# Filter spectra in DRAM: eight frequencies stored inside each lag, one 8 KB piece per Toeplitz row

## The chip, the cores and the metric

The kernel runs on one core of one Trainium2 chip. The metric is device time in microseconds of the whole launch; the median of three runs of the kernel before is 2986.34 us. TensorE is called PE below, VectorE DVE, ScalarE ACT, GpSimd POOL and SyncE SP. DMAs are issued from the queues of SP, POOL and ACT, and sixteen DMA engines move the bytes.

## The reference

Two layers act on `x` of shape (2, 128, 64, 64), that is two samples of 4096 tokens with 128 channels.

- Layer 0: group norm, a 1x1 projection to q, k and v with 2-D rotary positions, attention with four heads over 4096 tokens, an output projection and a residual.
- Layer 1, first half: `t = t + softmax(n n^T) n` with `n = layernorm(t)`.
- Layer 1, second half, where the change lies: a spectral filter. Cut to its core:

```python
Vf = rfft(phi, n=8192, axis=0)                      # 16 filters over 4096 lags
U_plus  = irfft(Vf * rfft(u))[:4096]                # causal convolution, per filter and channel
U_minus = irfft(Vf * rfft(u * sign))[:4096] * sign
out = einsum('btkd,k,kde->bte', U_plus,  s, Mpp) + einsum('btkd,k,kde->bte', U_minus, s, Mpm)
out = out + sum_i  shift(u, i) @ M_u[i]             # three taps
t = t + out                                         # of the branch that the softmax picks
```

## The kernel before, in words

Layer 0 and the attention of layer 1 run first, up to about 1740 us. In the attention of sample 0 (`attend(0, ...)`, 1030 to 1390 us), small pieces of other work are stepped beside the score loop by a chain of generators: statistics, then `filters`, then `matrices`, then `normalise` of sample 1. Beside the attention of sample 1 runs `feed` of sample 0.

`filters16` computes the spectra. For each parity `s` of the lags it transforms the filters to 128 frequencies with two matmuls, and DVE fills a tile `tb` of 128 frequencies by 2 (high and low half-precision part `h`) by 2 (row kind `i`) by 992 values: 31 lags of 32 values each. The tile is stored to the DRAM tensor `tables16` by one DMA on SP (L893), with the frequency outermost. `tb` uses a buffer tag "raw" that has one buffer, so the second parity's `tb` can be written only when the first one's store has read it; the raw matrices `mu_raw` and every second `raw` tile of `matrices` come next in that same buffer.

The filter stage takes the rest of the run. It works on 64 steps: 2 samples, 2 output parities `ro`, 8 chunks `ch` of 16 frequencies, 2 lag parities `s`. A step has two halves of `NS` = 8 frequencies. For each half, `chunk16` loads a table tile `tt` and a token tile `ut`, both of 128 partitions. Their partitions are filled in eight groups of 16 (four `q`, two `ci`): eight DMAs of 128 KB on SP for `tt` (L1311) and eight of 32 KB on POOL for `ut` (L1319). A table DMA builds the Toeplitz structure by itself: partition number p of the group reads 16 lags beginning at lag p, so neighbouring partitions read almost the same bytes, and one partition gets eight pieces (one for each frequency) of 1 KB.

`convolve16` multiplies: 16 matmuls per step of 128 x 128 by 128 x 512, the weights from `ut` and the moving operand `tt[:, at, :]` (L1372). ACT makes a half-precision copy of each result (L1379) and DVE the remainder (L1380). `mix16` (L1388) multiplies these with the mixing matrices, 48 matmuls per step, and is stepped one step behind. Matmuls of this stage stay in the order written (`ordered`). Table tiles exist twice (even steps `tables_a`, odd steps `tables_b`), token tiles twice per half. So the loads of step n wait until the matmuls of step n-2 have read the tile.

SP takes its DMAs strictly in order. In the first 16 steps `feed` of sample 1 shares its queue (stores `rows<-uh` at L1168 and L1169, which wait for ACT and DVE, and `base<-oc` at L1150), and in the later steps `back` (loads `had<-base` at L1484, which wait for the DVE additions at L1502). The framework also gives SP's DMAs eight semaphores in rotation: a DMA waits for the one issued eight before it to land, so at most eight of SP's are under way. POOL has eight of its own.

Apart from what is pinned, the framework orders each engine's instructions at build time by a plan with its own durations; a changed DMA can so move instructions elsewhere.

Of the kernel before, what the change touches and what calls it, by code (L numbers as in the profile page):

```python
# [13 lines left out]
F16 = mybir.dt.float16  # L14
# [8 lines left out]
P = 128  # L23
# [11 lines left out]
NK = 16  # L35
# [3 lines left out]
BP = NI // 2  # L39
NF = P  # L40
NW = NF // 4
NDI = 2 * BP - 1
TROW = NDI * NK
DROWS = 2 * BP + 1
WC = 4
NCH = NW // WC

# [25 lines left out]
def conv_attn_hybrid(ctx: ExitStack, tc: tile.TileContext, io):  # L75
    nc = tc.nc

    const = ctx.enter_context(tc.tile_pool(name="const", bufs=1))
    dram = ctx.enter_context(tc.tile_pool(name="dram", bufs=1, space=bass.MemoryType.DRAM))
# [27 lines left out]
    def pool(stack, name, bufs=1, **kw):  # L107
        return stack.enter_context(tc.tile_pool(name=name, bufs=bufs, reuse_waits="tile", **kw))
# [593 lines left out]

    tables = dram.tile([NF, 2, 2, 2 * TROW], F32, name="tables")
    rows = [dram.tile([2, DROWS, NF, C], F32, name=f"rows{b}") for b in range(B)]
    tables16 = dram.tile([NF, 2, 2, 2, 2 * TROW], F16, name="tables16")
    rows16 = [dram.tile([2, DROWS, 2, NF, C], F16, name=f"rows16_{b}") for b in range(B)]

    base = [dram.tile([C, NI, P], F32, name=f"base{b}") for b in range(B)]
# [42 lines left out]
    def network(layer0, in_halves):  # L751
        with ExitStack() as st:
            layers(st, layer0, in_halves)

    def layers(st, layer0, in_halves):
# [4 lines left out]
        px = pool(st, "px", side="right")  # L760
# [86 lines left out]
        def filters(p, fw):  # L847
            phi = p.tile([P, 2, TROW], F32, tag="phi", name="phi")
            nc.sync.dma_start(phi, io["phi"])
            yield  # L850
            if in_halves:
                yield from filters16(p, fw, phi)
                return
            for s in range(2):
                tb = p.tile([P, 2, 2 * TROW], F32, tag="raw", name=f"tb{s}")
                tbr = tb.rearrange("w i (o c k) -> w i c o k", c=2, k=NK)
                for c in range(2):
                    ph = bank(f"ph{s}_{c}")[:, :TROW]
                    nc.tensor.matmul(ph, fw[:, c, :], phi[:, s, :], start=True, stop=True)
                    ph = ph.rearrange("w (o k) -> w o k", k=NK)  # L860
                    nc.vector.tensor_copy(tbr[:, 0, c], ph)
                    if c == 0:
                        nc.vector.tensor_copy(tbr[:, 1, 1], ph)
                    else:
                        nc.vector.tensor_scalar(tbr[:, 1, 0], ph, -1.0, None, ALU.mult)
                    yield
                nc.sync.dma_start(tables[:, s], tb)

        def filters16(p, fw, phi):

            most = p.tile([P, 4, NK], F32, name="phi_most")
            for s in range(2):
                tb = p.tile([P, 2, 2, 2 * TROW], F16, tag="raw", name=f"tb{s}")
                tbr = tb.rearrange("w h i (o c k) -> w h i c o k", c=2, k=NK)
                for c in range(2):
                    ph = bank(f"ph{s}_{c}")[:, :TROW]
                    nc.tensor.matmul(ph, fw[:, c, :], phi[:, s, :], start=True, stop=True)
                    nc.vector.tensor_reduce(
                        most[:, 2 * s + c, :], ph.rearrange("w (o k) -> w k o", k=NK), AX.X, ALU.max,
                        apply_absolute_value=True,  # L880
                    )
                    ph = ph.rearrange("w (o k) -> w o k", k=NK)
                    nc.vector.tensor_scalar(tbr[:, 0, 0, c], ph, T_SCALE, None, ALU.mult)
                    nc.vector.scalar_tensor_tensor(
                        tbr[:, 1, 0, c], ph, T_SCALE, tbr[:, 0, 0, c], ALU.mult, ALU.subtract
                    )
                    for h in range(2):
                        if c == 0:
                            nc.vector.tensor_copy(tbr[:, h, 1, 1], tbr[:, h, 0, 0])
                        else:  # L890
                            nc.vector.tensor_scalar(tbr[:, h, 1, 0], tbr[:, h, 0, 1], -1.0, None, ALU.mult)
                    yield
                nc.sync.dma_start(tables16[:, s], tb)  # L893
            each = p.tile([P, NK], F32, name="phi_each")
            nc.vector.tensor_reduce(each, most.rearrange("p n k -> p k n"), AX.X, ALU.max)
            yield
            pt = bank("phi_most")
            nc.tensor.transpose(pt[:NK, :P], each, ident)
            col = p.tile([NK, 1], F32, name="phi_col")
            nc.vector.reduce_max(col, pt[:NK, :P], axis=AX.X)  # L900
            yield
            pt = bank("phi_row")
            nc.tensor.matmul(pt[0:1, :NK], col, ident[:NK, :NK], start=True, stop=True)
            ends = p.tile([1, 2], F32, name="phi_ends")
            nc.vector.tensor_reduce(ends[:, 0:1], pt[0:1, :NK], AX.X, ALU.max)
            nc.vector.tensor_reduce(ends[:, 1:2], pt[0:1, :NK], AX.X, ALU.min)
            nc.vector.tensor_scalar(ranges[:, 3:4], ends[:, 0:1], 1.0 / T_MOST, None, ALU.mult)
            nc.vector.tensor_scalar(ranges[:, 4:5], ends[:, 1:2], -1.0, 1.0 + T_LEAST, ALU.mult, ALU.add)
            yield
# [366 lines left out]
        late_pool = pool(right1, "late", 2, side="right")  # L1276

        if in_halves:
            pair = px.tile([P, 2, NF // NCH // 2, 2 * BP * NK], F16, tag="a", name="tables_a")
            tables_in = [  # L1280
                [pair[:, 0], pair[:, 1]],
                [px.tile([P, NF // NCH // 2, 2 * BP * NK], F16, tag=f"b{n}", name=f"tables_b{n}") for n in range(2)],
            ]
        else:
            tables_in = [
                px.tile([P, 2, WC // 2, 2 * BP * NK], F32, tag=f"b{n}", name=f"tables_in{n}") for n in range(2)
            ]

        def ordered(instruction):
            return tc.keep_in_program_order(instruction)  # L1290
# [4 lines left out]
        STREAM = {(0, 0): 0, (0, 1): 2, (1, 0): 1, (1, 1): 0}  # L1295
        FIRST = (0, BP + 1, BP)

        NS = NF // NCH // 2

        def chunk16(n, b, ro, ch, s):  # L1300

            row = FIRST[STREAM[ro, s]]
            halves = []
            for half in range(2):
                w0 = 2 * NS * ch + NS * half
                tt = tables_in[n % 2][half]
                ut = pf.tile([P, NS, C], F16, tag=f"tokens{half}", name=f"tokens{half}_{n}", bufs=2)
                for q in range(4):
                    for ci in range(2):
                        part = slice(32 * q + BP * ci, 32 * q + BP * ci + BP)  # L1310
                        nc.sync.dma_start(  # L1311
                            tt[part, :, :],
                            bass.AP(
                                tensor=tables16.tensor,
                                offset=tables16.offset + (((w0 * 2 + s) * 2 + q % 2) * 2 + ci) * 2 * TROW,
                                ap=[[2 * NK, BP], [16 * TROW, NS], [1, 2 * BP * NK]],
                            ),
                        )
                        nc.gpsimd.dma_start(  # L1319
                            ut[part, :, :], rows16[b][ci, row : row + BP, q // 2, w0 : w0 + NS, :]  # L1320
                        )
                halves.append((tt, ut))
            return halves
# [39 lines left out]
        def convolve16(u, halves, xh, xl):  # L1363

            for w in range(WC):
                tt, ut = halves[w // 2]
                pus = []
                for g2 in range(2):
                    pu = pc.tile([P, 2, 512], F32, tag="cv", name=f"cv{u}_{w}_{g2}", bufs=3)
                    for h in range(2):  # L1370
                        at = 4 * (w % 2) + 2 * g2 + h
                        ordered(nc.tensor.matmul(pu[:, h, :], ut[:, at, :], tt[:, at, :], start=True, stop=True))  # L1372
                    pus.append(pu)
                yield
                for g2, pu in enumerate(pus):
                    at = 128 * w + 64 * g2
                    pur = pu.rearrange("d h (c k) -> d k h c", k=NK)
                    hi, lo = (x[:, :, at : at + 64].rearrange("d k (h c) -> d k h c", h=2) for x in (xh, xl))
                    nc.scalar.copy(hi, pur)  # L1379
                    nc.vector.tensor_tensor(lo, pur, hi, ALU.subtract)  # L1380
# [146 lines left out]
        for b in range(B):  # L1527
            for ro in range(2):
                oh = (late_pool if ro else tokens[0]).tile(
                    [P, L], F32, tag="oh" if ro else "t", name=f"oh{b}_{ro}", bufs=1  # L1530
                )
                for ch in range(NCH):
                    acc = pc.tile([P, 512], F32, tag="acc", name=f"m{b}_{ro}_{ch}")
# [156 lines left out]
```

## Time and profile before

| | |
|---|---|
| Median of 3 runs | 2986.34 us (2985.1 to 2992.89) |
| Profiled execution | 2976.57 us, span on the core 2974.7 us |
| PE busy | 2731.7 us (92% of the span) |
| ACT, DVE, POOL busy | 1911.4, 1719.8, 648.2 us |
| Filter stage, 1740 to 2975 us | PE busy 1046.13 of 1235 us |
| Table loads | 2 x 512 DMAs of 128 KB, median 7.4 and 7.5 us from issue to landing |
| Token loads | 1024 DMAs of 32 KB, median 7.2 us to landing |

The busy shares are averages over stages with different limits. A group's idle time is the time its engine stood still just before it; what is named behind it is what ended that wait. The DMA share counts the time that pieces are under way, so it can exceed 1 when pieces overlap, and a high share does not tell which part of the path is full.

### The profile page before, as it was taken

To read this page: it belongs to the slowest core of one execution; us is meant where nothing else is said; L and a number is where in the kernel's file an instruction comes from. 1 tells how busy PE (TensorE), PEld (TensorE's weight loads), DVE (VectorE), ACT (ScalarE), POOL (GpSimd) and SP (SyncE) were. 2 spreads that over 40 slices of the span, in tenths; PEclk is the share of its full clock that TensorE was granted. 3 is DMA by queue.
4 is the path that set the end of the run, shared out by engine and by line. 5 is a ranking of instruction groups with operands and counts; after the bars stand their busy time and mean duration, and the time that the engine had idled before them with its cause. 6 is when DMAs were issued, how large, how long until landed. Compare 5 with 4: busy or idle time off the path is not lost.

```text
span 2974.7 us, 37241 instructions
## 1 busy us (share of the span) xinstructions
PE 2731.7 (92%) x12857; PEld 1372.3 (46%) x12857; DVE 1719.8 (58%) x2998; ACT 1911.4 (64%) x2507; POOL 648.2 (22%) x1313
## 2 busy tenths in 40 slices
PE   6999999999999999999999968888879987898898
PEld 3555555555455544554555523333344443344344
DVE  5264662364252389879866755554546654565564
ACT  4999999999999955665556643443435543453453
POOL 2022120021000010001000023333335543454341
PEclk9999999999999999999999978998999998999999
DMA  4122220021000014000210069999999989998995
GB/s 138 30 78 60 65 59 6 19 84 26 5 7 4 29 52 124 3 1 15 59 35 10 1 70 133 127 137 132 145 134 188 192 140 149 157 198 130 143 174 120
DMA packets 277542, 251.24 MB, mean 84 GB/s; under 512 B 79729, under 2 KB 241793, under 8 KB 277345
## 3 DMA queue, kind: packets, MB, share of 16 engines
q1 hardware_dynamic: 233536, 194.72, 40.0%
q0 software_dynamic: 40816, 50.82, 9.6%
q10 hardware_dynamic: 2992, 3.22, 0.3%
q8 instruction: 107, 1.75, 0.3%
q14 instruction: 91, 0.74, 0.1%
HBM read 210.37 MB, written 21.30 MB: 78 GB/s over the span
## 4 chain that ended last, share of the span: by engine, by line
PE 62%; DMA 21%; DVE 7%; ACT 7%; issue 2%; SPq 1%; POOL 0%; ACTq 0%; DVEq 0%; POOLq 0%
PE acc L206 12%; PE s L206 12%; PE m L1388 11%; DMA tables_a<-tables 9%; PE oacc L1055 9%; DMA tables_b<-tables 9%; ACT e L462 5%; PE y L1025 5%; PE cv L1372 4%; PE eT L1045 3%; PE ar L1146 1%; PE pf L1162 1%; DVE x L1380 1%; DMA tokens<-rows 1%; DVE eT L1048 1%
## 5 line engine op out<-in xcount | busy, mean ns | idle before, releaser
L462 ACT ACTIVATE e<-s 128x1536 f16<-128x1536 f32 (+1 forms) x704 | 937.0, 1428 | 33.7 <-PE s L206 28.8
L1379 ACT CAST x<-cv 128x1024 f16<-128x1024 f32 x512 | 493.4, 1015 | 562.6 <-PE cv L1372 562.0
L1380 DVE TENSOR_TENSOR x<-cv,x 128x1024 f16<-128x1024 f32 x512 | 603.1, 1220 | 422.2 <-ACT x L1379 422.2
L1319 POOL DMA_DIRECT2D tokens<-rows x1024 | 491.0, 485 | 679.4 <-DMA tokens<-rows 313.3
L1388 PE MATMUL m<-x,mxr 128*128 128x512 f16 x2048 | 629.1, 384 | 0.0
L206 PE MATMUL s<-qs,ks 128*128 128x512 f16 x2048 | 558.4, 380 | 7.4 <-ACT e L462 3.8
L206 PE MATMUL acc<-e,v 128*97 128x512 f16 x2048 | 557.5, 379 | 3.3 <-DVE accs L410 0.2
L1388 PE MATMUL m<-x,mxl 128*128 128x512 f16 x1024 | 399.3, 390 | 1.0 <-DVE oh L1395 1.0
L206 PEld LDWEIGHTS <-v 128*97 128x97 bf16 x2048 | 254.8, 124 | 214.7 <-issue 12.6
L1388 PEld LDWEIGHTS <-mxr 128*128 128x128 f16 x2048 | 203.0, 99 | 249.3 <-issue 14.8
L1034 ACT ACTIVATE ey<-y,nshift 128x512 f32<-128x512 f32 x288 | 195.6, 688 | 185.3 <-PE y L1025 137.8
L206 PEld LDWEIGHTS <-ks 128*128 128x128 f16 x2048 | 200.6, 99 | 227.6 <-issue 43.9
L1025 PE MATMUL y<-bothT 128*128 128x512 f16 x864 | 223.8, 379 | 1.4 <-ACT ey L1034 1.4
L1372 PEld LDWEIGHTS <-tokens 128*128 128x128 f16 x1024 | 98.9, 100 | 262.4 <-issue 132.6
L1372 PE MATMUL cv<-tables_a,tokens 128*128 128x512 f16 x512 | 139.6, 397 | 68.9 <-DMA tokens<-rows 26.2
L1055 PE MATMUL oacc<-ep,hi 128*128 128x512 f16 x576 | 191.3, 379 | 8.0 <-DVE ep L1087 6.5
L1048 DVE TENSOR_TENSOR eT<-eT,eT 128x512 f16<-128x512 f32 x224 | 147.4, 684 | 88.3 <-ACT eT L1047 87.2
L410 DVE COPY accs<-acc 97x512 f32<-97x512 f32 x64 | 44.2, 691 | 259.9 <-PE acc L206 259.9
L1087 DVE TENSOR_TENSOR ep<-ey,ep 128x512 f16<-128x512 f32 x288 | 191.4, 684 | 5.2 <-PE oacc L1055 0.7
L1372 PE MATMUL cv<-tables_b,tokens 128*128 128x512 f16 x512 | 139.1, 396 | 59.1 <-DMA tokens<-rows 33.5
L1047 ACT ACTIVATE eT<-eT 128x512 f16<-128x512 f32 x224 | 132.9, 603 | 65.8 <-PE eT L1045 64.8
L1388 PEld LDWEIGHTS <-mxl 128*128 128x128 f16 x1024 | 103.1, 101 | 133.1 <-issue 16.0
(215 smaller groups left out, 2567.1 us busy)
## 6 DMA issues: line engine op xcount, KB each, us to landing
tables_a<-tables SPq DMA_DIRECT2D x512, 128.0 KB, 7.4
tables_b<-tables SPq DMA_DIRECT2D x512, 128.0 KB, 7.5
tokens<-rows POOLq DMA_DIRECT2D x1024, 32.0 KB, 7.2
tab<-in_rot SPq DMA_DIRECT2D x32, 512.0 KB, 4.1
rows<-uh SPq DMA_DIRECT2D x128, 64.0 KB, 1.7
ks<-term POOLq DMA_DIRECT2D x112, 64.0 KB, 2.2
qs<-term POOLq DMA_DIRECT2D x112, 64.0 KB, 2.1
accs<-back SPq DMA_DIRECT2D x32, 128.0 KB, 2.3
```

Of the source, the lines that this page charges most:

```text
L206: tc.keep_in_program_order(nc.tensor.matmul(*args, **kw))
L462: nc.scalar.activation(e[:, own, :], ps[:, own, :], AF.Exp, scale=SCORE_SCALE)
L1025: nc.tensor.matmul(ps[:, q, :], a[0][:, bass.ts(t, P)], c[0][:, bass.ts(i, 512)], start=(n == 0), stop=(n == 2),)
L1034: nc.scalar.activation(e[:, 2 * h + q, :], ps[:, q, :], AF.Exp, bias=nshift16 if in_halves else nshift, accum_out=den[:, t, i : i + 1],)
L1048: nc.vector.tensor_tensor(eT[1], pt, eT[0], ALU.subtract)
L1055: nc.tensor.matmul(acc, a[0][:, own], c, start=(start and t == 0 and n == 0), stop=(stop and t == len(es) - 1 and n == 2),)
L1087: nc.vector.tensor_tensor(es[t][1], e[:, t, :], es[t][0], ALU.subtract)
L1319: nc.gpsimd.dma_start(ut[part, :, :], rows16[b][ci, row : row + BP, q // 2, w0 : w0 + NS, :])
L1372: ordered(nc.tensor.matmul(pu[:, h, :], ut[:, at, :], tt[:, at, :], start=True, stop=True))
L1379: nc.scalar.copy(hi, pur)
L1380: nc.vector.tensor_tensor(lo, pur, hi, ALU.subtract)
L1388: nc.tensor.matmul(acc, m, x, start=(s == 0 and i == 0), stop=(s == 1 and i == len(products) - 1))
```

## The change

`tables16` gets another order of its dimensions: parity, high or low part, row kind, block of eight frequencies, lag, frequency within the block, 32 values. A group's partition then reads its 16 lags of all eight frequencies as one contiguous piece of 8 KB, and partitions follow at 512 bytes instead of 64. The number of table loads, their size, their destination partitions and their queue stay.

In exchange the store of a `tb` tile becomes 64 DMAs on SP (2 parts, 2 row kinds, 16 blocks), each from 8 partitions in pieces of 64 bytes. In SBUF the table tile has the lag outside the frequency, so the moving operand of a convolution matmul is no longer 1 KB in a row, but 16 runs of 64 bytes, 512 bytes apart. The changed lines:

```diff
-    tables16 = dram.tile([NF, 2, 2, 2, 2 * TROW], F16, name="tables16")
+    tables16 = dram.tile([2, 2, 2, NF // NS, NDI, NS, 2 * NK], F16, name="tables16")
...
-                nc.sync.dma_start(tables16[:, s], tb)
+                for h in range(2):
+                    for i in range(2):
+                        for b in range(NF // NS):
+                            nc.sync.dma_start(
+                                tables16[s, h, i, b].rearrange("o w x -> w o x"),
+                                tb[NS * b : NS * b + NS, h, i, :].rearrange("w (o x) -> w o x", x=2 * NK),
+                            )
...
-            pair = px.tile([P, 2, NF // NCH // 2, 2 * BP * NK], F16, tag="a", name="tables_a")
+            pair = px.tile([P, 2, BP, NS, 2 * NK], F16, tag="a", name="tables_a")
...
+                        own = tables16[s, q % 2, ci, w0 // NS]
                         nc.sync.dma_start(
-                            tt[part, :, :],
+                            tt[part],
                             bass.AP(
-                                tensor=tables16.tensor,
-                                offset=tables16.offset + (((w0 * 2 + s) * 2 + q % 2) * 2 + ci) * 2 * TROW,
-                                ap=[[2 * NK, BP], [16 * TROW, NS], [1, 2 * BP * NK]],
+                                tensor=own.tensor,
+                                offset=own.offset,
+                                ap=[[NS * 2 * NK, BP], [1, BP * NS * 2 * NK]],
                             ),
                         )
...
-                        ordered(nc.tensor.matmul(pu[:, h, :], ut[:, at, :], tt[:, at, :], start=True, stop=True))
+                        ordered(nc.tensor.matmul(pu[:, h, :], ut[:, at, :], tt[:, :, at, :], start=True, stop=True))
```

`NS` (8) moves to the head of the file, and `tables_b` gets the same new shape.

More of the change, by code (lines that the diff above doesn't have):

```diff
@@ L46 @@
 NCH = NW // WC
+NS = NF // NCH // 2
 QK_SCALE = 256.0
@@ L1278, in layers @@
         if in_halves:
-            pair = px.tile([P, 2, NF // NCH // 2, 2 * BP * NK], F16, tag="a", name="tables_a")
+            pair = px.tile([P, 2, BP, NS, 2 * NK], F16, tag="a", name="tables_a")
             tables_in = [
                 [pair[:, 0], pair[:, 1]],
-                [px.tile([P, NF // NCH // 2, 2 * BP * NK], F16, tag=f"b{n}", name=f"tables_b{n}") for n in range(2)],
+                [px.tile([P, BP, NS, 2 * NK], F16, tag=f"b{n}", name=f"tables_b{n}") for n in range(2)],
             ]
@@ L1296, in layers @@
         FIRST = (0, BP + 1, BP)
-        NS = NF // NCH // 2
         def chunk16(n, b, ro, ch, s):
```

## The prediction

> **What bounds the kernel now.** I read the page's slices first, then the filter stage by windows, then SP's own waits, then the DMA view of short windows.
>
> ```profile
> PE   6999999999999999999999968888879987898898
> DMA  4122220021000014000210069999999989998995
> GB/s 138 30 78 60 65 59 6 19 84 26 5 7 4 29 52 124 3 1 15 59 35 10 1 70 133 127 137 132 145 134 188 192 140 149 157 198 130 143 174 120
> ```
>
> Until slice 23 PE is full and the DMA engines nearly idle. From there to the end, PE has gaps and the DMA row stands at 9. Windows of that stage (length, busy PE, PEld, DVE, ACT, POOL, granted clock, DMA share, GB/s):
>
> ```profile
> 2100.00:2225.00 125.00, 100.13 (x467) 49.74 (x466) 61.81 (x58) 46.24 (x51) 47.45 (x99) 0.92 1.05 137
> 2225.00:2425.00 200.00, 196.75 (x924) 90.45 (x923) 136.10 (x118) 109.50 (x117) 106.77 (x223) 1.00 1.09 184
> 1740.00:2975.00 1235.00, 1046.13 (x4667) 482.72 (x4665) 683.91 (x672) 527.08 (x576) 492.97 (x1026) 0.93 1.02 149
> ```
>
> There are two regimes. In the first row PE waits and a step of 64 matmuls takes 17 to 20 us (from one step's first table issue to the next's). In the second PE is full, a step takes about 13.5 us (924 matmuls in 196.75 us are 0.213 us each, times 64), and the same DMA engines move more bytes. Over the stage PE idles 1235 - 1046 = 189 us. Its named waits on loads are:
>
> ```profile
> PE cv L1372 <- DMA tokens<-rows: 59.7, 17, 10.3
> PE cv L1372 <- DMA tables_b<-tables: 40.3, 14, 17.4
> PE cv L1372 <- DMA tables_a<-tables: 23.1, 13, 7.2
> SPq L1311 <- DMA tables_a<-tables: 277.8, 412, 2.3
> SPq L1311 <- DMA tables_b<-tables: 265.2, 403, 2.5
> ```
>
> Together 123 us of PE (us, times, longest). SP waits for its own earlier loads nearly all the time, so the tables are the backlog. The question is what makes a table load slow. Two windows of the DMA view (its GB/s row in 40 parts; the first holds only `m<-mx`, L1266; the second only tables, as the stage starts; tokens join at its end):
>
> ```profile
> GB/s 0 0 0 0 0 0 0 0 113 133 31 51 82 215 338 369 348 307 328 348 307 399 379 369 410 348 277 93 0 0 0 0 0 0 0 0 0 0 0 0
> m<-mx SPq DMA_DIRECT2D x2, 256.0 KB, 2.7
> GB/s 110 146 95 123 123 115 126 123 113 131 110 108 141 97 120 126 113 126 123 97 138 105 118 133 108 123 123 105 128 123 100 126 118 120 128 113 118 126 102 118
> tables_a<-tables SPq DMA_DIRECT2D x12, 128.0 KB, 8.8
> ```
>
> Both move pieces of 1 KB on the same queue. `m<-mx`, into 128 partitions, reaches 300 to 400 GB/s, in its packet records 46 ns a piece. The tables, into 16 partitions at a time, hold 118 GB/s flat: 131072 bytes in 1.11 us. In the trace's packet records the first pieces of the first table loads also take 46 ns, and only after about 1 us 100 to 200 ns: the reading keeps up until something behind it is full. So 1 KB is not what slows them; the destination is.
>
> [...] No strided moving operand stands in this trace.
>
> **The change, part by part.**
>
> Table loads. 1024 stay, of 128 KB, to the same 16 partitions, on the same queue in the same order (in the changed kernel's instruction order SP differs only by the stores). Bytes through the destination are equal, so I take the pace as equal: 1.11 us each where they bound, 0.75 us in the stretch where PE bounds. Cost 0. If 16 pieces instead of 128 do matter, the best is that all 123 us go; the worst is in the rivals. The nearest row for long pieces shared by partitions is `accs<-back`, 128 KB in 2.3 us to landing, but it is alone on the DMA engines and goes to 32 partitions.
>
> Convolution matmuls. 1024 with 64-byte runs. I take 0[...].
>
> Stores. Two DMAs become 128. The nearest rows are `rows<-uh` (L1168, L1169): 256 pieces each, SP busy 0.36 to 0.47 us, 1.7 us to landing; a new store has 8 x 31 = 248 pieces. Eight under way at 1.7 us would allow one each 0.2 us, so SP's issue sets the pace: 64 x 0.42 = 27 us. The first `tb` is complete at 1082.07 us, where the old store was issued; so the last new one leaves near 1109 and lands near 1111, where the old one was done in 3.8.
>
> Who waits: the second `tb` has the same buffer, and its first DVE write waits for all 64. In the changed order, DVE has about 16 us of other work ahead of it (14 attention operations at some 0.6 us, 25 of 0.15 to 0.35 us for the branch weights, 16 coefficients in 2.2 us, three reductions), so it arrives at about 1098 and stands until 1111. Queued behind it on DVE are eight `tb` operations (3.4 us) and then the `eT` remainders, without which PE can't go on: it has two banks for the `eT` transposes. PE has in its order some 55 matmuls and the transposes ahead of that point, up to about 1099. It then stands until about 1114: 15 us. Of these, 2 us I give back, since the matrix work of DVE that follows moves to a time with more room (DVE 17.7 to 19.9 of 20 us busy between 1100 and 1220, 13 to 16 after). So **+13 us**; 0 if the plan's slack covers it, 20 if each store takes 0.5 us.
>
> The second 64 stores end at about 1145; `mu_raw` and `raw0` wait for them, but stand some 110 DVE instructions (80 us) later in the new order, and the matrices still come ahead of sample 1's `normalise`. Nothing else is in SP's queue then. Cost 0. Small pieces into DRAM could be dearer than these rows: [...] 31 pieces at 46 ns would make 1.4 us a store, 91 us a set, and the wait about 80 us.
>
> Sum: 2976.57 + 13 = 2990 for the profiled execution. The median of the runs stands 9.8 us above the profiled one, so the forecast is **2999 us**. A measurement of this kernel tells about 0.3%, 9 us, from no change.
>
> **Rivals.**
>
> 1. *The likeliest*: pace unchanged, the stall of the stores added: 2999. Some 38 steps are bound by loads at about 17.7 us; 3% of pace is 20 us either way: 2979 to 3019.
>
> 2. *Slower by more*: long pieces cost the overlap. In the full stretch the loads exceed the 118 GB/s, so there the DMA engines must be at different loads[...], and the trace shows this: from first to last of a load's sixteen completions pass about 0.6 us at the stage's start and 2.4 to 3 us in that stretch. An 8 KB piece is a DMA engine's whole share of a load[...]. If this holds the engines in step, the 25 or so fast steps fall to 18 us: 25 x 4.5 = 113, with the stores 3112. It decides once the stretch delivers under 2.62 MB in 13.5 us, 194 GB/s. For: the pace at the start, when all go in step. Against: tokens have slack (POOL also waits 302.5 us for free tiles). Dear stores or strided operands end here too: about 3070 to 3100.
>
> 3. *Faster*: what fills is the handling of many pieces into few partitions. Then the loads hide and PE sets the pace: 123 us of waits go, and up to 35 us more as the granted clock (0.93 in the stage) returns to 1.00: 2999 - 123 = 2876, at best 2840. For: the pieces are eight times longer. Against: the 46 ns above.
>
> 4. *The change does nothing to the loads and the stores are hidden*: 2986. It is the low end of case 1.
>
> **How the numbers follow.** Case 1 (with 4) 0.46, case 2 with dear stores and operands 0.34, case 3 0.20. Range 2870 to 3115: it takes in the upper half of case 3 and most of case 2. Faster by over 0.3%: case 3 and a sliver of case 1, 0.22. Within: a fifth of case 1, 0.10. Slower: 0.68.
>
> **What would show it.** In the profile after: the DMA view at the stage's start again near 118 GB/s, with pieces of 8 KB; table loads landing in 7 us or more; PE idle about 190 us in the stage; a DVE wait at the second `tb` of 10 to 15 us near 1100, and PE's with it; matmul duration at L1372 still 379 ns at the median. I am wrong if tables land in 3 to 5 us and PE's waits for them vanish (case 3), if no slice of the stage exceeds 150 GB/s (case 2), if the stores take over 0.6 us each, or if cv matmuls are longer.

## The result, and the profile after

The changed kernel takes 3005.48 us (median of 20 runs, 2990.17 to 3039.46), the kernel before 2985.72 us on the same chip: a ratio of 1.0085, 95% interval 1.0058 to 1.0112 (ratios here are of undisturbed runs on one chip, medians are of all runs, so the two can differ by some tenths of a per cent). It is slower, close to the 2999 us forecast. The profile shows that this is the sum of two changes: the filter stage became some 45 us shorter, where the forecast had 0, and it starts 78.5 us later, where the forecast had 13.

The changed kernel's slices (span 3006.4 us, so 75 us each):

```profile
PE   6999999999999979099999996888989997899898
DMA  4021220030000020400111006989799987997994
GB/s 138 27 83 53 69 54 6 26 83 19 6 5 6 27 26 6 142 3 1 25 53 34 4 1 104 139 134 143 144 141 164 212 166 136 159 206 139 154 200 104
```

PE was at 9 in slices 1 to 22 before. Now slice 14 shows a 7 (1052 to 1127 us) and slice 16 a 0 (1203 to 1278 us). The last 16 slices are the filter stage. Windows of the changed kernel: length, busy PE, PEld, DVE, ACT, POOL, granted clock, DMA share, GB/s:

```profile
1080.00:1120.00 40.00, 22.95 (x106) 12.39 (x105) 24.12 (x76) 11.96 (x35) 0.60 (x1) 0.79 0.34 41
1204.00:1280.00 76.00, 1.35 (x6) 0.80 (x6) 46.39 (x120) 0.00 (x0) 0.10 (x1) 0.53 0.46 139
1816.30:3006.00 1189.70, 1040.05 (x4680) 483.53 (x4678) 685.79 (x675) 529.02 (x582) 493.15 (x1026) 0.93 0.89 154
```

The kernel before in the first of these windows, and in the one where its matrix steps ran:

```profile
1080.00:1120.00 40.00, 36.43 (x176) 18.25 (x174) 37.16 (x109) 18.04 (x53) 0.74 (x2) 0.91 0.32 110
1108.00:1188.00 80.00, 71.28 (x341) 35.22 (x341) 75.48 (x185) 42.85 (x121) 0.00 (x0) 0.94 0.39 116
```

In the first window PE is busy 13.5 us less than before (22.95 for 36.43). In the second, 1204 to 1280 us, PE does next to nothing, while DVE works 46.39 us of it. In the third PE idles 150 us (1189.7 - 1040.05), where it was 189. The waits of the changed kernel (us in total, times, longest) name what PE and DVE stand for:

```profile
PE mx_most L1011 <- DVE mx_top L1008: 74.6, 1, 74.6
PE cv L1378 <- DMA tokens<-rows: 53.7, 17, 15.3
PE cv L1378 <- DMA tables_b<-tables: 29.5, 9, 9.9
...
PE eT L1052 <- DVE tb L885: 17.0, 1, 17.0
...
PE cv L1378 <- DMA tables_a<-tables: 2.7, 3, 1.0
...
DVE pm L748 <- DMA raw<-in_mpm: 23.1, 15, 4.1
...
DVE tb L884 <- DMA tables<-tb: 10.1, 1, 10.1
```

(The lines moved by six or so: L1378 are the `cv` matmuls, L1011 the last matmul of `matrices`.) PE's waits on tables and tokens together fell from 123 to 86 us. The waits on tables alone fell from 63.4 to 32.2 us, but in four later profiles with the same loads they are 44 to 64 (84 to 102 with tokens), so only the sum is read, and that roughly. The stall at the second `tb` is there, 10.1 us on DVE and 17.0 us on PE. And there is one wait of 74.6 us that no step of the forecast has. The timeline of the changed kernel (start, duration, engine, line) at the end of that wait:

```profile
1274.08 0.42 DVE L1000 TENSOR_REDUCE mx_most<-raw 128x1 f32<-128x256 f32 x1
1275.55 0.35 DVE L748 TENSOR_SCALAR pm<-raw,coef 128x256 f32<-128x256 f32 x1 [1.06 <-DMA raw<-in_mpm]
...
1278.48 0.17 DVE L1008 TENSOR_REDUCE mx_top<-mx_most 128x1 f32<-128x16 f32 x1
1278.80 0.58 PE L1011 MATMUL mx_most<-ident,mx_top 128*1 128x128 f32 x2 [74.65 <-DVE mx_top L1008]
```

DVE runs the sixteen matrix steps one after the other, with no attention operation between them. Each takes about 4.2 us, of which mostly 1.1 to 1.5 us is waiting for the next `raw`, which can be loaded only when one of the two buffers is free. PE has the small `mx_most` matmul ahead of its attention work in its own order, so it stands until the sixteenth step is done. Before, the same steps stood between the attention operations (1108 to 1188 us), and PE was busy for 71.28 of those 80 us.

**Theory A.** Two effects of opposite sign: the loads gain some 45 us in the stage; the 128 stores lose some 79 us ahead of it, a little through the shared buffer and mostly because the matrix steps fall into one block. **Rivals**: the shorter stage comes from the later start or another alignment of the queues (B); the matrix block costs the same wherever the stores are (C); the shared buffer is the whole cause (A2).

### The profile page after: what moved, and what is told of

It reads as the page before. It is cut to its first block, busy times and chain, and to the rows that moved or that the text cites. A ratio compares the mean times of both kernels' runs of the same rounds, so it can differ in the third digit from the quotient of the medians.

```text
span 3006.4 us, 37428 instructions
## 1 busy us (share of the span) xinstructions
PE 2722.6 (91%) x12857; PEld 1374.9 (46%) x12857; DVE 1732.6 (58%) x2998; ACT 1911.8 (64%) x2507; POOL 648.3 (22%) x1313
## 4 chain that ended last, share of the span: by engine, by line
PE 68%; DMA 15%; DVE 7%; ACT 7%; issue 2%; SPq 1%; POOL 0%; ACTq 0%; DVEq 0%; POOLq 0%
PE m L1394 14%; PE acc L207 11%; PE s L207 11%; PE oacc L1062 10%; ACT e L463 5%; PE y L1032 5%; PE cv L1378 5%; DMA tokens<-rows 4%; DMA tables_b<-tables 4%; PE eT L1052 3%; DMA tables_a<-tables 3%; DMA raw<-in_mpm 2%; PE ar L1153 2%; DVE x L1386 1%; PE pf L1169 1%
## 5 line engine op out<-in xcount | busy, mean ns | idle before, releaser
L1378 PEld LDWEIGHTS <-tokens 128*128 128x128 f16 x1024 | 100.0, 100 | 218.2 <-issue 87.0
L1378 PE MATMUL cv<-tables_a,tokens 128*128 128x512 f16 x512 | 137.9, 393 | 47.6 <-DMA tokens<-rows 39.8
L1378 PE MATMUL cv<-tables_b,tokens 128*128 128x512 f16 x512 | 137.4, 392 | 41.2 <-DMA tables_b<-tables 25.0
```

The source lines that it names most:

```text
L1378: ordered(nc.tensor.matmul(pu[:, h, :], ut[:, at, :], tt[:, :, at, :], start=True, stop=True))
```

## Experiments: the loads and the stores apart

**1. The changed loads alone**

```diff
-                for h in range(2):
...
+                nc.sync.dma_start(
+                    tables16[s].rearrange("h i b o w x -> (h i b o w x)").rearrange("(p y) -> p y", p=P),
+                    tb.rearrange("w h i x -> w (h i x)"),
+                )
```

> The changed loads alone. The tables keep the changed shape in DRAM and are loaded in 8 KB pieces with the strided matmul operand, but each tb leaves in one store as before, so the frequencies and lags stand permuted in DRAM and the output is not the reference's. Theory A (two effects that cancel: the loads gain in the filter stage, the 128 stores lose ahead of it): the stage takes about 1190 us as in the changed kernel (before 1235), it starts at about 1738 as before, and the time is about 45 us under before: 2930 to 2950. Theory B (the shorter stage is owed to the later start or to another alignment of the two queues, and the pieces do nothing): stage 1235, time within 10 us of before, 2976 to 2996.

Measured: 2928.17 us, ratio 0.9853 (0.9804 to 0.9903), that is 44 us of 2986, and just under the range of A. The first table load is issued at 1737.7 us, as before. Its window of the stage:

```profile
1737.70:2925.70 1188.00, 1035.44 (x4680) 481.56 (x4678) 685.74 (x675) 529.08 (x582) 495.27 (x1026) 0.94 0.90 155
```

1188 us with the start of before (1237 then): the loads shorten the stage by themselves. B falls.

**2. The stores alone**

```diff
                 nc.sync.dma_start(tables16[:, s], tb)
+                for h in range(2):
+                    for i in range(2):
+                        for b in range(16):
+                            nc.sync.dma_start(
+                                copy16[s, h, i, b].rearrange("o w x -> w o x"),
...
```

> The kernel before, with the 128 small stores added beside its own two stores: they fill a second tensor that nothing reads. Loads, matmuls and table layout are those of before. Theory A: the stage starts about 78 us later (near 1816) for two stalls of PE, some 10 to 14 us near 1100 and some 65 to 75 us near 1204 to 1279 where DVE has its sixteen matrix steps in one block; the stage stays at about 1235; time 3050 to 3070. Theory B (the 75 us come from something else in the changed kernel, not from the stores): only the first stall, time 2990 to 3005.

Measured: 3051.68 us, ratio 1.0288 (1.0220 to 1.0357), 86 us. DVE's instructions stand in the order of the changed kernel, the matrix steps in one block, and the waits of this kernel are those of the changed one:

```profile
PE mx_most L1012 <- DVE mx_top L1009: 74.1, 1, 74.1
...
PE eT L1053 <- DVE tb L885: 20.8, 1, 20.8
```

The stage starts at 1819.9 us, 82 us late. It lasted 1216 us in this profile, less than before with the same loads: one profile's stage wanders by some 20 us, and the medians decide. The two halves add to 0.9853 + 1.0288 - 1 = 1.0141, with half widths of 0.5% and 0.7%; the whole change, 1.0085, agrees.

**3. Stores after the matrices, own buffers for `tb`**

```diff
-                tb = p.tile([P, 2, 2, 2 * TROW], F16, tag="raw", name=f"tb{s}")
+                tb = p.tile([P, 2, 2, 2 * TROW], F16, tag=f"tb{s}", name=f"tb{s}", bufs=1)
...
-                steps = chain(left, stats.steps(), filters(p, fw), matrices(p), normalise(1, stats, stage, gate))
+                steps = chain(left, stats.steps(), filters(p, fw), matrices(p), store_late(), normalise(1, stats, stage, gate))
```

> The changed kernel with a buffer of its own for each tb, and the 128 stores issued after the matrices, so that no DVE write and no load of mu_raw or raw stands behind them. Theory A: no DVE wait at the second tb, the matrix steps stand between attention steps again, the stage starts within 15 us of 1738 and lasts about 1190: time 2930 to 2955, below before. Theory C (the matrix block costs the same wherever the stores are, since the raw loads pace it): start stays near 1800, time 2990 to 3005.

Measured: 2935.19 us, ratio 0.9873 (0.9823 to 0.9924). The stage starts at 1740.0 us (and lasts 1207 in this profile, not the 1190 expected). The same 128 stores cost next to nothing here; of the block, in DVE's order only the last two or three steps of the sixteen still stand without attention work between, and PE waits for them:

```profile
PE mx_most L1018 <- DVE mx_top L1015: 8.2, 1, 8.2
```

C falls. This version computes all of the reference and beats both kernels.

**4. Own buffers alone**

```diff
-                tb = p.tile([P, 2, 2, 2 * TROW], F16, tag="raw", name=f"tb{s}")
+                tb = p.tile([P, 2, 2, 2 * TROW], F16, tag=f"tb{s}", name=f"tb{s}", bufs=1)
```

> The changed kernel with a buffer of its own for each tb and nothing else moved: the stores are issued where they were. In the program's order the sixteen matrix steps still stand in one block on DVE, though mu_raw moves ahead. Theory A1 (the block itself costs the 65 to 75 us, because the raw loads are planned behind the 128 stores in SP's queue, shared buffer or not): only the first stall goes, 10 to 14 us, and the time is 2988 to 2998. Theory A2 (the shared buffer is the whole cause): both stalls go, the stage starts near 1738, time 2920 to 2945.

Measured: 2986.53 us, ratio 1.0030 (1.0002 to 1.0058), just under the range of A1; start at 1791.1 us, 25 us earlier than the changed kernel and 53 later than before. The wait at `tb` is gone, the block stays. PE's wait, then SP's stores and first raw loads, then DVE's first matrix step:

```profile
PE mx_most L1011 <- DVE mx_top L1008: 65.1, 1, 65.1
...
1085.00 54.34 SPq L897 DMA_DIRECT2D tables<-tb  x128
1139.44 0.41 SPq L985 DMA_DIRECT2D raw<-in_mpp  x1
...
1188.77 0.35 DVE L748 TENSOR_SCALAR pm<-raw,coef 128x256 f32<-128x256 f32 x1
```

So A1 holds in the main: the shared buffer costs the 17 us at `tb` and some 10 of the block (`mu_raw` and `raw` arrive earlier), the block itself the rest. It comes from the program's order, which was planned with the raw loads and the `mx` stores behind 128 stores in SP's queue. On the chip the stores are done long before: here the first raw matrices are loaded right behind them, at 1139 us, and DVE reaches the first step 49 us later, without a wait for them.

**5. The stores from POOL's queue, own buffers**

```diff
-                            nc.sync.dma_start(
+                            nc.gpsimd.dma_start(
                                 tables16[s, h, i, b].rearrange("o w x -> w o x"),
```

> The changed kernel with a buffer of its own for each tb and the 128 stores issued by POOL instead of SP, at the same place. In the program's order the matrix steps stand between attention steps again. Theory A (the stores hurt only by what stands behind them in SP's queue and by the shared buffer): stage starts within 10 us of 1738, time 2925 to 2945, as with the late stores or a little under. Theory F (POOL is slower at issuing, and the reciprocal root of sample 1's statistics, which POOL computes, waits behind 128 stores[...]): stage starts 20 us or more later than 1738, time 2950 to 2980.

Measured: 2947.15 us, ratio 0.9823 (0.9765 to 0.9882); start at 1745.8 us, 8 us late. POOL's group of these stores (busy us, mean ns):

```profile
L897 POOL DMA_DIRECT2D tables<-tb x128 | 89.7, 704 | 9.2 <-DVE tb L884 8.8 <-issue 0.4
```

0.7 us each instead of SP's 0.43, and it matters little: DVE has its matrix steps between attention operations again, since none of the matrix loads and stores stands behind them. F falls. Versions 3 and 5 can't be told apart by these intervals.

## Experiments: what makes a table load slow

Theory P: each piece of a load into few partitions costs a fixed time, so eight times fewer pieces are the gain.

**6 and 7. Pieces of 2 and 4 KB** (as experiment 1, but with two or four frequencies inside a lag; here two):

```diff
-    tables16 = dram.tile([2, 2, 2, NF // NS, NDI, NS, 2 * NK], F16, name="tables16")
+    tables16 = dram.tile([2, 2, 2, NF // 2, NDI, 2, 2 * NK], F16, name="tables16")
...
-                                ap=[[NS * 2 * NK, BP], [1, BP * NS * 2 * NK]],
+                                ap=[[2 * 2 * NK, BP], [NDI * 2 * 2 * NK, NS // 2], [1, BP * 2 * 2 * NK]],
```

> As the kernel of the changed loads alone (one store for each tb, the DRAM contents permuted, the output not the reference's), but with two frequencies inside each lag where that has eight: pieces of 2 KB, 64 to a load. Theory P (a fixed time is spent on each piece of a load into few partitions): the time saved grows with the share of pieces removed, one half here against seven eighths, so the saving is 4/7 of that of 8 KB (44 us): about 25 us, 2955 to 2970. Theory Q (only a piece that is a DMA engine's whole share of a load helps[...]): no saving, 2978 to 2992.

> The same with four frequencies inside each lag: pieces of 4 KB, 32 to a load (permuted, output not the reference's). Theory P: three quarters of the pieces are gone, the saving is 6/7 of that of 8 KB, about 38 us: 2940 to 2958. Theory Q: no saving, 2978 to 2992.

Measured: 0.9846 (0.9797 to 0.9895) and 0.9822 (0.9776 to 0.9868); with 8 KB it was 0.9853 (the kernel before took 3002 us on this chip, so only the ratios are compared). Q falls at once. P asks for a gain that grows with the piece; its 25 us at 2 KB would be a ratio of about 0.992, outside the interval. That counts against P and doesn't rule it out, since the 8 KB gain it starts from is itself known only to a third. By the medians the whole gain is there with the first doubling.

**8. The changed layout, pieces of 1 KB**

```diff
-            pair = px.tile([P, 2, BP, NS, 2 * NK], F16, tag="a", name="tables_a")
+            pair = px.tile([P, 2, 8, 520], F16, tag="a", name="tables_a")
...
-                                ap=[[NS * 2 * NK, BP], [1, BP * NS * 2 * NK]],
+                                ap=[[NS * 2 * NK, BP], [512, 8], [1, 512]],
```

> As the kernel of the changed loads alone (changed layout in DRAM, one store for each tb, contents permuted, output not the reference's), but each tables tile has 16 bytes of gap after every 1 KB, so that the same bytes go to the same 16 partitions in the same order in 128 pieces of 1 KB instead of 16 of 8 KB. The matmul reads nearly the same 64-byte runs. Theory P (the length of a piece is what the changed loads gain by): the gain is lost, time within 12 us of before (ratio 0.996 to 1.004), pieces at the stage's start near 158 ns in the median. Theory L (the new order of the data in DRAM or SBUF is the gain, the pieces are not): ratio 0.982 to 0.990 as with 2, 4 and 8 KB.

Measured: 0.9892 (0.9858 to 0.9926). With 128 pieces a load, as before, three quarters of the gain remain by the medians, and the interval leaves out both "no gain" and P's range. So the order of the data gives much of the gain by itself. Whether the pieces give the rest, the times do not resolve.

The pace of the loads tells more. The first tokens move 18 us after the first table load; until then tables have the DMA engines to themselves. The DMA view of 16 us there (1740 to 1756 us, in this run 1740.4 to 1756.4) for the kernel before, for this run and for experiment 1:

```profile
DMA packets 2083, 1.89 MB, mean 118 GB/s; under 512 B 234, under 2 KB 2083, under 8 KB 2083
```

```profile
DMA packets 2187, 2.00 MB, mean 125 GB/s; under 512 B 248, under 2 KB 2186, under 8 KB 2186
```

```profile
DMA packets 529, 2.16 MB, mean 135 GB/s; under 512 B 265, under 2 KB 265, under 8 KB 265
```

118 to 125 GB/s is the order of the data at an equal piece. From there pieces of 2, 4 and 8 KB reach 126, 128 and 135 (135 to 139 in five traces with 8 KB, 118 to 122 in three of the old order). In the packet records a piece takes 158 ns before, 155 in this run, and 271, 521 and 968 with 2, 4 and 8 KB: 136, 130 and 121 ns for each KB. So longer pieces do have a share here, of P's kind, and by this measure it is the larger one. Over a longer stretch it fades: up to the 385th table load (24 steps) the old order took 517 to 526 us in three traces, the new one 500 with 1 KB, 508 and 507 with 2 and 4 KB, 496 to 505 with 8 KB. L holds for a part of the gain, and in the whole stage, as the times say, for most of it; the exact split stays open. Which order it is stays open too: the layout changes where a load reads in DRAM (a partition's bytes adjacent, where its eight pieces lay 15.9 KB apart; a piece begins at a multiple of 512 bytes, where it was 64) and in which order SBUF is written and read, and no run parts these.

**9. Token pieces of 1 KB, the kernel before**

```diff
-                ut = pf.tile([P, NS, C], F16, tag=f"tokens{half}", name=f"tokens{half}_{n}", bufs=2)
+                ut = pf.tile([P, 2, NS // 2 * C + 16], F16, tag=f"tokens{half}", name=f"tokens{half}_{n}", bufs=2)
```

> The kernel before, with a gap of 32 bytes in the middle of each tokens row in SBUF, so that token pieces are of 1 KB like the table pieces, twice as many. Theory T (what 2 KB table pieces gained was their share against the token pieces[...]): equal pieces gain as much, ratio 0.980 to 0.990, PE's waits on tables (63.4 us) fall by half and those on tokens (59.7 us) do not grow by as much. Theory P (a time for each piece): 16384 pieces more, no gain: ratio 0.998 to 1.015.

Measured: 1.0026 (0.9988 to 1.0064). No gain: the tables' share against the tokens is not what changed. T falls. The result fits P's range, which a cost of nothing fits as well.

**10. The destination: a column of 128 partitions**

```diff
-                            tt[part, :, :],
+                            tt[:, 2 * q + ci, :],
...
-                                ap=[[2 * NK, BP], [16 * TROW, NS], [1, 2 * BP * NK]],
+                                ap=[[2 * NK, P], [1, 2 * BP * NK]],
```

> The kernel before (pieces of 1 KB, 128 to a load, same bytes, same queue, same number of loads), but each table load is written to one column of all 128 partitions instead of to eight columns of 16 partitions. The matmuls then read other data and the output is not the reference's. Theory D (the 16 partitions of the destination bound the load, as the prediction had it): loads run at 250 GB/s or more where nothing else limits, PE's waits on tables go, the stage takes 1060 to 1120 us and the time is 2850 to 2890. Theory E (the time of a DMA engine on each 1 KB piece bounds the load, wherever it goes): stage and time as before, 2976 to 2996.

Measured: 2757.70 us, ratio 0.9197 (0.9153 to 0.9242), beyond D's range on the fast side. Its window of the stage, and its DMA view from 1738 to 1754 us:

```profile
1736.10:2753.50 1017.40, 985.64 (x4680) 474.14 (x4678) 685.33 (x675) 526.05 (x582) 492.65 (x1026) 0.99 0.63 181
```

```profile
GB/s 266 272 266 297 312 248 154 287 295 256 307 167 284 310 305 190 218 259 97 0 0 0 0 0 0 0 41 259 284 200 287 313 246 261 225 248 246 289 243 254
...
tables_a<-tables SPq DMA_DIRECT2D x12, 128.0 KB, 2.7
```

The same number of loads, bytes and 1 KB pieces, and mostly 250 to 310 GB/s while loads are under way, instead of 118. In the packet records a table piece takes 46 ns in the median (158 before). PE's waits on tables are gone, PE idles 32 us in the stage instead of 189, and the granted clock is 0.99 instead of 0.93. The same 4680 matmuls take 986 us of PE instead of 1048, in the ratio of the two clocks; that gives the last 60 us. The matmuls work on other data here, and no run parts that from the end of the waits as the reason for the higher clock. These loads also read neighbouring rows, so the order of reading differs too; what speaks for the destination is that before, the first pieces of the first loads took 46 ns as well, in the old order, for some 0.8 us (1738.8 to 1739.6 us), ahead of the median of 158.

**11 and 12. Rows of 64 partitions**, a try to use this with all of the reference computed. First the kernel before with 64 KB loads; then version 3 with 512 KB loads:

```diff
+                            tt[64 * r : 64 * r + 64, at, :],
...
+                                ap=[[2 * TROW, 4], [2 * NK, BP], [1, 2 * BP * NK]],
```

```diff
+                        tt[64 * r : 64 * r + 64],
...
+                            ap=[[NF * TROW * 2, 4], [NS * 2 * NK, BP], [1, BP * NS * 2 * NK]],
```

> The kernel before with its two stores and its layout in DRAM, but each half step of tables comes in 16 loads of 64 KB, each the four (part, component) pairs of one frequency, to 64 partitions in pieces of 1 KB, instead of 8 loads of 128 KB to 16 partitions. It computes all of the reference. Theory D (the number of partitions written at once bounds a load): loads run at 200 GB/s or more where nothing else limits (256 to 313 were seen into 128 partitions, 118 into 16), PE's waits on tables go, the stage takes 1020 to 1080 us, time 2760 to 2830. Theory G (twice as many loads cost as much in issue and completion as they gain: 1024 more at 0.3 us of SP's time and at least as much in waits for earlier loads): 2900 to 2990.

> The changed kernel with the late stores (own buffers for tb, stores after the matrices), and with each half step of tables loaded in 2 loads of 512 KB to 64 partitions, in pieces of 8 KB, instead of 8 loads of 128 KB to 16 partitions. It computes all of the reference. The rows of 64 partitions before it were held by SP, 507 ns of issue and a wait for each 64 KB, while pieces took 46 ns; here SP issues 256 loads in all, 130 us at that price, so issue can't bind. Theory D (the number of partitions written at once bounds a load): 8 KB pieces near 310 ns instead of 968, loads at 200 GB/s or more, PE's waits on tables go, the stage takes 1020 to 1080 us, time 2750 to 2815. Theory H (64 partitions are no better a destination than 16, the slow part of the last run was its own destination too): stage 1190 to 1240 as with the late stores, time 2930 to 2990.

Measured: 3426.23 us (1.1438, 1.1382 to 1.1494) and 3279.16 us (1.0946, 1.0889 to 1.1004). Both theories of each fail. The queue line (packets, MB, share of 16 engines) of a 16 us window at the stage's start, of the first and of the second:

```profile
q1 hardware_dynamic: 1316, 1.27, 24.6%
```

```profile
q1 hardware_dynamic: 162, 1.26, 24.8%
```

A quarter of sixteen engines, both times, where the kernel before had 116.9%. In the packet records exactly four pieces are under way for some 70% (first) and 90% (second) of the time (16 and more before), and a piece is quick: 46 ns for 1 KB in the median, as in experiment 10, and about 320 ns for 8 KB (968 in experiment 1). Four at a time without a gap would give 4 x 1024 B / 46 ns = 89 GB/s and 4 x 8192 B / 320 ns = 102 GB/s; the windows show 82 and 87, tokens included. My reading of the first of the two, that SP's 507 ns of issue held it, was wrong: the second issues 256 table loads instead of 2048 and keeps four pieces under way all the same. What sets the four was not shown. Both runs have an outermost dimension of 4 in the loads' pattern (16 in the table loads so far, 128 in experiment 10) and 64 partitions to write to, and no run parts the two. So these two runs leave 64 partitions as a destination open. Loads with the 16 lags outermost, and the token rows permuted to match, were not tried.

## Why the prediction was right in its total and wrong in two terms

- **First stall, +13 us: right.** Predicted: DVE stands 13 us and PE 15. Measured: 10.1 and 17.0 us, PE busy 13.5 us less between 1080 and 1120. The 128 stores went out in 55.8 us, 0.43 each, where 0.42 was costed.
- **"The second 64 stores ... Cost 0": wrong, and the larger error.** The prediction saw that `mu_raw` and the raw tiles come later, and measured that against sample 1's `normalise`, the consumer of the data. It did not ask what else stands with them. In the new order the sixteen steps were one block without an `eT` remainder, and PE had `mx_most` ahead of its attention work. Cost: 74.6 us of PE in the changed kernel, 74.1 with the stores alone, 65.1 with own buffers, 8.2 or nothing where the order is mixed. Some 10 us come back, since DVE is less full elsewhere (between 1108 and 1188 us it is busy for 53.7 us instead of 75.5, and PE for 76.7 instead of 71.3): 13.5 + 74.6 - 10 is the 78.5 us of the later start. The "2 us I give back" was that term, too small.
- **"Table loads ... Cost 0": wrong, -44 us.** "Bytes through the destination are equal, so I take the pace as equal" is the step that failed. That the destination limits is borne out (118 GB/s into 16 partitions, mostly 250 to 310 into 128 in experiment 10, as far as its other order of reading allows), but a load so limited still changes pace: 118 to 125 GB/s with the order of its data, to 135 with longer pieces as well (experiments 8 and 1). "So 1 KB is not what slows them" went too far with it. Predicted signs that failed with it: 118 GB/s at the stage's start (140 in the changed kernel from 1818 to 1834 us) and 190 us of idle PE (150).
- **Convolution matmuls, 0: right.** The 0 was my estimate, which the trace of before did not show. Measured: 379 ns in the median before and after, with the operand in runs of 64 bytes; the means fell from 397 to 393 ns.
- **Slower rival, the lost overlap: did not come.** The stage still has slices of 206 and 212 GB/s. That long pieces hold the engines in step was my estimate; no view shows it, and table and token pieces of equal length gained nothing (ratio 1.0026, experiment 9). **Faster rival: its direction was in the loads, its mechanism was not.** Many pieces are not the main thing that fills, since 1 KB pieces in the new order keep most of the gain in time; they have a share in the pace at the stage's start. About a third of its 123 us came.
- **The total was luck.** It was 6 us off because -44 and about +66 (78.5 less the 13 predicted) largely cancel, with what one profile's stage and the runs' spread leave. Either half alone would have missed it: 2928 or 3052.
- Two smaller readings of the working are off, with nothing resting on them: SP waits for its own loads 543 of 1235 us, which is not "nearly all the time", and a load in the stretch where PE bounds takes 13.5 / 16 = 0.84 us, not 0.75.

## What to carry to other kernels

A DMA that becomes many can cost less by its own issue than by what a build-time plan then puts behind it (here 13 to 17 us against 65 to 75): read the new order on each engine around the move, and ask for each block which other in-order engine waits at its end. A transfer limited by its destination is no reason to expect an equal pace when the layout changes (here 118 GB/s, then 125 with equal pieces and 135 with longer ones). When a large edit moves the time little, run its halves alone: here one gained 1.5%, the other lost 2.9%, and moving the stores out of the way kept the gain (0.982 to 0.987 of before).

## What the runs showed of the hardware that I had not expected

- 128 KB in 1 KB pieces: 118 GB/s into 16 partitions, mostly 250 to 310 GB/s into 128 (with another order of reading), the piece 158 and 46 ns.
- At 16 partitions the order of the data changes the pace (118 to 125 GB/s at 1 KB, tables alone under way). The length of a piece, 1 to 8 KB, changes it too (125, 126, 128, 135 GB/s), but the kernel's time shows no trend with it (ratios 0.9892, 0.9846, 0.9822, 0.9853).
- Loads into 64 partitions with an outermost dimension of 4 in their pattern: four pieces under way for some 70% and 90% of the time (16 and more before), and in experiment 11 the issue of such a load on SP takes 507 ns in the median instead of 303.
- A store of 8 partitions in 64-byte pieces takes SP 0.43 us from one to the next, POOL 0.70 us.
